# One late exponential per pair of key tiles, scores in groups of four, and one weight tile of 104 made without ScalarE

## The chip, the core and the metric

The kernel runs on one core of a Trainium2 chip. The metric is the device time of one execution in microseconds (us); of several runs the median is taken. The engines are called as in the profile: PE (TensorE matrix multiplication; PEld is its loading of weights), DVE (VectorE), ACT (ScalarE), POOL (GpSimd) and SP (SyncE, which issues nearly all DMAs here).

## What is computed

Four graph layers follow each other on 3327 nodes with 128 features, each of the form `x = x + layer(relu(layernorm(x)))`. Layers 0, 2 and 3 multiply by a 3327 x 3327 adjacency matrix of zeros and ones. Nearly all of the time goes to layer 1, an attention with a softmax for each of the 128 features:

```python
q = (x @ Wq.T).reshape(d, n, h)      # d = 128 softmaxes, n = 3327 nodes, h = 8
k = (x @ Wk.T).reshape(d, n, h)
v = (x @ Wv.T).reshape(d, n, h)
a = jnp.einsum('dnh,dmh->dnm', q, k) * scale
a = a + spatial_encoding + edge_encoding     # both are adj
a = jax.nn.softmax(a, axis=2)
out = jnp.einsum('dnm,dmh->dnh', a, v)
```

So 128 matrices of 3327 x 3327 exponentials are needed, `exp(q.k + 2 adj)`. The kernel calls each of the 128 a head.

## The kernel before

**Tiles.** Keys lie in 26 tiles of 128 partitions (`T = 26`), queries in seven chunks of 476 columns (`QW`; the last has 471), heads in 32 groups of four. The attention loop runs over chunks, in them over groups, in them over key tiles: 7 x 32 x 26 = 5824 steps, 2912 pairs of an even and an odd step. The order of the instructions on every engine is that of the code (a manual schedule), and each engine works through its own in that order; it stops at the first that has to wait.

**A step** (`scores`, then `weigh` of the step four before, `ahead = 4`). For each of four heads PE multiplies 32 rows (8 features in split precision) of keys and queries into a score tile of 128 keys x 476 queries in PSUM (L547). The four heads use four different groups of 32 rows of the array. Twice the adjacency (`a2`, bf16) is then brought in by one of three ways, named by a letter in `WAYS`:

- D: VectorE adds `a2` to the score tile and writes it to the weights `p8` (L552). These tiles are called `early`; four PSUM buffers of that name are used in turn. ScalarE takes the exponential of all five D tiles of a pair with one wide instruction of 5 x 476 columns (L557), in the odd step.
- I: PE adds `a2` to the score tile itself by a product with an identity matrix (L550), and ScalarE takes the exponential straight from PSUM (L553).
- G: ScalarE takes the exponential of the scores alone from PSUM (L553), and GpSimd multiplies by a stored `exp(a2)` (L555).

The I and G tiles are called `late`. An even step has the ways D D D I and one late tile, an odd one D D I G and two; each kind has one PSUM buffer (`late1`, `late2`, three banks in all). With four banks for `early` and one for the sum, the eight banks are full. A score matmul that writes `late` waits until ScalarE has read the last one there.

**Weighing.** `weigh` multiplies the four weight tiles of a step by the values (L564), each into its own group of 32 columns of the array, and sums over the key tiles in one PSUM bank. In the trace it shows as eight matmul records for a step, two passes for each head. After the last key tile VectorE copies the sum out (L573).

**Beside it.** The next group's keys, queries and values are loaded at step 4 (`load_heads`, L392), GpSimd casts two key tiles at a time from step 13 on (`key_pair`, L419). In the first chunk GpSimd also splits keys and queries of later groups into two parts (`Parting`). While one chunk is worked on, the adjacency of the next is loaded, doubled by GpSimd (L272), and stored; in a chunk's last group ScalarE makes the 13 tiles of its exponential (L347).

**Before attention** PE projects `q`, `k` and `v` for 26 row tiles; ScalarE copies them to staging buffers (`qk_st` L466, `v_st` L474), and SP stores them to DRAM. GpSimd sets a column of ones in each `v_st` first (L473). Between the rows a list `early` of prepared steps is worked off, among them the parting of groups 0 and 1 and the whole loading of the first four heads in one step.

Of the kernel before, what the change touches and what calls it, by code (L numbers as in the profile page):

```python
# [1 line left out]

# [6 lines left out]
F32 = mybir.dt.float32  # L9
F32R = mybir.dt.float32r  # L10
# [3 lines left out]
I32 = mybir.dt.int32  # L14
U32 = mybir.dt.uint32
AF = mybir.ActivationFunctionType
ALU = mybir.AluOpType
# [4 lines left out]
P = 128  # L22
N = 3327
D = 128
T = 26
NP = P * T
NH = 128
E = 8
EA = E + 1
HL = 2 * E  # L30
GP = NP * NH
QW = 476
# [22 lines left out]
def kernel(  # L55
# [23 lines left out]
    nc = tc.nc  # L79
# [183 lines left out]
    a_first = []  # L263
# [74 lines left out]
    kq = ctx_at.enter_context(tc.tile_pool(name="at_kq", bufs=2))  # L338
    e_pool = ctx_at.enter_context(tc.tile_pool(name="at_e", bufs=T // 2 + 1))

    def even(c):
        w = q_chunks[c][1]
        return w + w % 2

    def exp_of(a2, c):
        e = e_pool.tile([P, QW], F32, name="e")
        nc.scalar.activation(e[:, : even(c)], a2[:, : even(c)], AF.Exp)  # L347
        return e
# [7 lines left out]
    class Parting:  # L356


        def __init__(self, g):
            self.g, self.hi, self.lo = g, [None] * 2, [None] * 2  # L360
# [22 lines left out]
        def at(self, t):  # L383

            for side in range(2):
                t0 = 2 + 4 * side
                if t0 <= t < t0 + 4:
                    self.part(side, t - t0)
                if t == 11:
                    self.store(side)  # L390

    def load_heads(c, g):  # L392
        q0, w = q_chunks[c]
        k_in = kq.tile([P, NP], F32, name="k_in", bufs=1)
        q4 = kq.tile([P, QW], F32R, name="q4")
        v4 = kq.tile([P, 4, T, EA], F32, name="v4")
        nc.gpsimd.memset(k_in[:, N:], 0.0)
        if w % 2:
            nc.gpsimd.memset(q4[:, w : w + 1].bitcast(F32), 0.0)
        for i in range(4):  # L400
            n0 = (4 * g + i) * N
            for j in range(2):
                r = 32 * i + HL * j
                nc.sync.dma_start(k_in[r : r + HL, :N], kt[:, n0 : n0 + N])
                nc.sync.dma_start(q4[r : r + HL, :w].bitcast(F32), dram(qt, E * j * GP + n0 + q0, [[0, 2], [GP, E], [1, w]]))
        for i in range(4):
            n0 = (4 * g + i) * N
            nc.sync.dma_start(
                v4[:, i].rearrange("p t e -> p (t e)"),
                vd[n0 : n0 + NP, :].rearrange("(p t) e -> p (t e)", t=T),  # L410
            )
        return k_in, q4, v4, []

    def key_pair(heads):

        k_in, _, _, pairs = heads
        t = 2 * len(pairs)
        k = kq.tile([P, 2, P], F32R, name="k", bufs=T)
        nc.gpsimd.tensor_copy(k, slots(k_in)[:, t : t + 2, :])  # L419
        pairs.append(k)  # L420

    with tc.tile_pool(name="l1", bufs=1) as pool, tc.tile_pool(name="l1_ps", bufs=3, space=PSUM) as ps:
# [13 lines left out]
        st = ctx_st.enter_context(tc.tile_pool(name="l1_st", bufs=4))  # L436
# [7 lines left out]
        early = []  # L444
        for g in range(2):
            part = Parting(g)
            for side in range(2):
                early.append(lambda part=part: (part.load(0), part.load(1)) if part.lo[0] is None else None)
                early.append(lambda part=part, side=side: [part.part(side, i) for i in range(4)] and part.store(side))
        first, e_first = [], []  # L450
        early.append(lambda: first.extend(load_heads(0, 0)))
        ahead_part = Parting(2)
        early.append(lambda: (ahead_part.load(0), ahead_part.load(1)))
        early.append(lambda: e_first.extend(exp_of(a, 0) for a in a_first[1::2]))
        early += [lambda: (key_pair(first), key_pair(first))] * (T // 4)
        if T // 2 % 2:
            early.append(lambda: key_pair(first))
        for r in range(T):
            kp = rows_of(r)
            lhs = hT[:, r * P : r * P + kp]  # L460
            for i, (dst, mx) in enumerate(((qf, q_max), (kf, k_max))):
                pp = ps.tile([P, 2, 512], F32, name="pp", bufs=2)
                for c in range(2):
                    nc.tensor.matmul(pp[:kp, c, :], lhs, w_st[:, i, c * 512 : c * 512 + 512], start=True, stop=True)
                s = st.tile([P, E * NH], F32, name="qk_st")
                nc.scalar.activation(s[:kp], pp[:kp].rearrange("p a b -> p (a b)"), AF.Copy, scale=D**-0.5 if i == 0 else 1.0)  # L466
                nc.vector.tensor_reduce(mx[:kp, r : r + 1], s[:kp], AX.X, ALU.max, apply_absolute_value=True)
                store(dst[:E].rearrange("e (r c) -> r e c", c=NH), s.rearrange("p (e c) -> p e c", c=NH), r, kp)
            pp = ps.tile([P, 2, 512], F32, name="pp", bufs=2)
            for c in range(2):  # L470
                nc.tensor.matmul(pp[:kp, c, :], lhs, w_st[:, 2, c * 512 : c * 512 + 512], start=True, stop=True)
            s = st.tile([P, NH, EA], F32, name="v_st")
            nc.gpsimd.memset(s[:, :, E : E + 1], 1.0)  # L473
            nc.scalar.copy(s[:kp, :, :E], pp[:kp].rearrange("p a (c e) -> p (a c) e", e=E))  # L474
            store(vd.rearrange("(r c) e -> r (c e)", c=NH), s.rearrange("p c e -> p (c e)"), r, kp)

            if r > 1 and early:
                early.pop(0)()
# [23 lines left out]

    WAYS = ("DDDI", "DDIG")
    PLACES = ((0, 1, 2, 5), (3, 4, 6, 7))
    two_i = const.tile([P, P], BF16, name="two_i")
    nc.vector.tensor_copy(two_i, ident)
    engines = {
# [5 lines left out]
    }  # L515
    n_groups = NH // 4
    ahead = 4
    adj_pools.append(ctx_at.enter_context(tc.tile_pool(name="at_adj1", bufs=T)))
    with tc.tile_pool(name="at_in", bufs=1) as a_pool, tc.tile_pool(name="at_p", bufs=3) as p_pool, tc.tile_pool(
        name="at_ps", bufs=1, space=PSUM  # L520
# [12 lines left out]
            q0, w = q_chunks[c]  # L533
            nc.sync.dma_start(adj16[t][:, q0 : q0 + w], a2[:, :w])

        def scores(step, heads, a2, e_a, p8):
            c, _, t = step
            we = even(c)
            _, q4, _, pairs = heads
            ways, places = WAYS[t % 2], PLACES[t % 2]  # L540
            n_d = ways.count("D")
            late = ps.tile([P, 4 - n_d, 512], F32, name=f"late{4 - n_d}")
            early = [ps.tile([P, 512], F32, name="early", bufs=4) for _ in range(n_d)]
            for i in (*range(n_d, 4), *range(n_d)):
                r = slice(32 * i, 32 * i + 32)
                sp = early[i] if i < n_d else late[:, i - n_d]
                nc.tensor.matmul(sp[:, :we], pairs[t // 2][r, t % 2, :], q4[r, :we], start=True, stop=ways[i] != "I")  # L547
            for i in range(4):
                if ways[i] == "I":
                    nc.tensor.matmul(late[:, i - n_d, :we], two_i, a2[:, :we], start=False, stop=True)  # L550
            for i in range(n_d):
                nc.vector.tensor_tensor(p8[:, places[i], :we], early[i][:, :we], a2[:, :we], op=ALU.add)  # L552
            nc.scalar.activation(p8[:, places[n_d] : places[3] + 1, :we], late[:, :, :we], AF.Exp)  # L553
            if ways[3] == "G":
                nc.gpsimd.tensor_tensor(p8[:, places[3], :we], p8[:, places[3], :we], e_a[:, :we], op=ALU.mult)  # L555
            if t % 2:
                nc.scalar.activation(p8[:, :5, :we], p8[:, :5, :we], AF.Exp)  # L557

        def weigh(step, v4, p8):
            c, g, t = step  # L560
            q0, w = q_chunks[c]
            kp = rows_of(t)
            for i in range(4):
                nc.tensor.matmul(  # L564
                    acc[32 * i : 32 * i + EA, :w],
                    v4[:kp, i, t, :],
                    p8[:kp, PLACES[t % 2][i], :w],
                    start=(t == 0),
                    stop=(t == T - 1),
                )  # L570
            if t == T - 1:
                o4 = a_pool.tile([P, QW], F32, name="o4")
                nc.vector.tensor_copy(o4[: 96 + EA, :w], acc[: 96 + EA, :w])  # L573
                for i in range(4):
                    n0 = (4 * g + i) * N + q0
                    nc.sync.dma_start(ot[:, n0 : n0 + w], o4[32 * i : 32 * i + EA, :w])

        with tc.manual_schedule(engines=engines):
            groups = [(c, g) for c in range(len(q_chunks)) for g in range(n_groups)]
            steps = [(c, g, t) for c, g in groups for t in range(T)]  # L580
            heads = first
# [4 lines left out]
            for j, step in enumerate(steps):  # L586
# [6 lines left out]
                        a_t, a_next = a_next, []  # L593
                        e_t, e_next = e_next, []
                if t % 2 == 0:
                    p8 = p_pool.tile([P, 8, QW], F32, name="p8")
                scores(step, heads, a_t[t], e_t[t // 2], p8)
                begun[j] = (step, heads[2], p8)
                if j >= ahead:
                    weigh(*begun.pop(j - ahead))  # L600
                if t == min(4, T // 2) and more:
                    coming = load_heads(*groups[n])
                if c == 0 and g + 2 < n_groups:
# [506 lines left out]
```

## Time and profile before

| | us |
|---|---|
| runs, median (lowest to highest of 3) | 11194.51 (11192.19 to 11195.0) |
| the profiled execution | 11195.14 |
| its span, first to last instruction | 11193.4 |
| attention in it: first exponential to last | 576 to 10471 |
| projection before it | 380 to 566 |

The profile is one execution. Of a group of equal instructions it gives the busy time, the mean duration of one and the idle time of its engine in front of them. Durations contain a start and a tail that overlap with the neighbours (two late exponentials and a wide one have means of 980, 1387 and 2609 ns, and yet they start again every 3.37 us), so throughput is read from start to start. PE's matmuls are pipelined and their ends are modelled; for PE, too, starts are what counts. PE's clock was granted in full during attention.

POOL's groups that matter: the product with `exp(a2)` takes 1212 ns, a cast of two key tiles 697 ns, doubling a tile with a tensor_scalar 1417 ns.

### The profile page before, as it was taken

To read this page: it belongs to the slowest core of one execution; us is meant where nothing else is said; L and a number is where in the kernel's file an instruction comes from. 1 tells how busy PE (TensorE), PEld (TensorE's weight loads), DVE (VectorE), ACT (ScalarE), POOL (GpSimd) and SP (SyncE) were. 2 spreads that over 40 slices of the span, in tenths; PEclk is the share of its full clock that TensorE was granted. 3 is DMA by queue.
4 is the path that set the end of the run, shared out by engine and by line. 5 is a ranking of instruction groups with operands and counts; after the bars stand their busy time and mean duration, and the time that the engine had idled before them with its cause. 6 is when DMAs were issued, how large, how long until landed. Compare 5 with 4: busy or idle time off the path is not lost. (4 is left out here: it accounts for less than half of the span.)

```text
span 11193.4 us, 209350 instructions
## 1 busy us (share of the span) xinstructions
PE 10850.5 (97%) x79530; PEld 3005.9 (27%) x79530; DVE 9343.1 (83%) x15429; ACT 10199.3 (91%) x9152; POOL 6016.3 (54%) x6964
## 2 busy tenths in 40 slices
PE   9899999999999999999999999999999999999996
PEld 4322222222222222222222222222222222222453
DVE  8588888888888888888888888888888888888656
ACT  0399999999999999999999999999999999999522
POOL 0277777555555555555555555555555555555203
PEclk9899999999999999999999999999999999999998
DMA  7755554333333333333333333333333332333432
GB/s 264 238 129 120 123 127 109 65 64 64 68 64 62 67 66 63 68 65 61 68 66 63 66 66 61 67 66 61 66 66 61 66 63 55 61 58 58 135 113 97
DMA packets 417541, 942.25 MB, mean 84 GB/s; under 512 B 67936, under 2 KB 345937, under 8 KB 380940
## 3 DMA queue, kind: packets, MB, share of 16 engines
q1 hardware_dynamic: 412762, 918.98, 37.4%
q8 instruction: 627, 10.27, 0.4%
q0 software_dynamic: 3760, 9.78, 0.3%
q14 instruction: 392, 3.21, 0.1%
HBM read 788.78 MB, written 139.71 MB: 83 GB/s over the span
## 5 line engine op out<-in xcount | busy, mean ns | idle before, releaser
L552 DVE TENSOR_TENSOR p<-early,a 128x476 f32<-128x476 f32 (+1 forms) x14560 | 8426.4, 646 | 1369.4 <-PE early L547 1297.5
L557 ACT ACTIVATE p<-p 128x2380 f32<-128x2380 f32 (+1 forms) x2912 | 7568.4, 2599 | 0.4
L564 PE MATMUL acc<-p,v 128*9 128x476 f32 (+1 forms) x46592 | 5748.5, 564 | 15.3 <-ACT p L557 1.4
L553 ACT ACTIVATE p<-late 128x476 f32<-128x476 f32 (+1 forms) x5824 | 5315.4, 1175 | 13.8 <-DMA q<-qt 10.2
L555 POOL TENSOR_TENSOR p<-p,e 128x476 f32<-128x476 f32 (+1 forms) x2912 | 3528.1, 1212 | 3204.3 <-ACT p L553 2998.6
L547 PE MATMUL late<-q,k 32*128 32x476 f32 (+1 forms) x8736 | 2798.2, 478 | 99.5 <-ACT p L553 39.7
L547 PE MATMUL early<-q,k 32*128 32x476 f32 (+1 forms) x14560 | 2843.6, 478 | 9.4 <-DVE p L552 9.4
L419 POOL CAST k<-k_in 128x256 fp32r<-128x256 f32 x2912 | 1936.5, 697 | 886.4 <-DMA k_in<-kt 339.4
L547 PEld LDWEIGHTS late<-q,k 32*128 32x128 f32 x8736 | 1065.4, 181 | 4890.4 <-ACT p L553 4186.2
L550 PE MATMUL late<-a,two_i 128*128 128x476 bf16 (+1 forms) x5824 | 2180.8, 374 | 0.0
L547 PEld LDWEIGHTS early<-q,k 32*128 32x128 f32 x14560 | 1113.0, 181 | 9.9 <-DVE p L552 9.9
L564 PEld LDWEIGHTS acc<-p,v 128*9 128x9 f32 x46592 | 695.2, 88 | 1272.6 <-issue 1185.8
L550 PEld LDWEIGHTS <-two_i 128*128 128x128 bf16 x5824 | 556.2, 96 | 1329.0 <-issue 1329.0
L189 ACT COPY agg<-agg_ps 128x512 f32<-128x512 f32 x15 | 8.2, 591 | 485.5 <-PE agg_ps L204 290.6
L230 PE MATMUL agg_ps<-a,part 128*128 128x512 bf16 (+1 forms) x1092 | 227.0, 369 | 4.3 <-ACT agg L928 3.2
L272 POOL TENSOR_SCALAR a<-a_in 128x476 bf16<-128x476 f32 (+2 forms) x156 | 221.1, 1417 | 0.5
L272 POOL TENSOR_SCALAR a<-a 128x476 bf16<-128x476 f32 (+1 forms) x26 | 36.4, 1400 | 288.1 <-DMA a<-in_adjT_dram 288.1
L923 PE MATMUL sp<-yT,hT 128*128 128x512 f32 (+1 forms) x364 | 170.7, 610 | 12.3 <-ACT agg L928 6.4
L204 PE MATMUL agg_ps<-a,h 128*128 128x512 f32 (+2 forms) x364 | 148.2, 570 | 26.2 <-DVE h L164 26.2
L573 DVE COPY o<-acc 105x476 f32<-105x476 f32 (+1 forms) x224 | 144.5, 645 | 4.6 <-PE acc L564 4.6
L204 PE MATMUL agg_ps<-a,x 128*128 128x512 f32 (+2 forms) x364 | 145.3, 562 | 0.6 <-ACT x L318 0.6
L230 PEld LDWEIGHTS <-part 128*128 128x128 f16 x1092 | 108.6, 99 | 117.7 <-issue 10.3
(236 smaller groups left out, 2592.0 us busy)
## 6 DMA issues: line engine op xcount, KB each, us to landing
k_in<-kt SPq DMA_DIRECT2D x1792, 207.9 KB
v<-vd SPq DMA_DIRECT2D x896, 117.0 KB
a<-in_adjT_dram SPq DMA_DIRECT2D x50, 1663.5 KB
a<-adj SPq DMA_DIRECT2D x78, 831.8 KB
q<-qt SPq DMA_DIRECT2D x1536, 29.8 KB
a_in<-in_adjT_dram SPq DMA_DIRECT2D x125, 238.0 KB
adj<-a SPq DMA_DIRECT2D x156, 119.0 KB
vd<-v_st SPq DMA_DIRECT2D x25, 576.0 KB
```

The costliest lines, as they stand in the source:

```text
L204: nc.tensor.matmul(acc[c][:, :w], lhs[:kp, t, :], a[:kp, c0 : c0 + w], start=(t == 0), stop=(t == T - 1))
L230: nc.tensor.matmul(acc[c][:, :w], part[:, t, :], a[:, c0 : c0 + w], start=(t == 0 and i == 0), stop=(t == T - 1 and i == len(parts) - 1),)
L272: nc.gpsimd.tensor_scalar(a2[:kp, :w], a, 2.0, None, op0=ALU.mult)
L419: nc.gpsimd.tensor_copy(k, slots(k_in)[:, t : t + 2, :])
L547: nc.tensor.matmul(sp[:, :we], pairs[t // 2][r, t % 2, :], q4[r, :we], start=True, stop=ways[i] != "I")
L550: nc.tensor.matmul(late[:, i - n_d, :we], two_i, a2[:, :we], start=False, stop=True)
L552: nc.vector.tensor_tensor(p8[:, places[i], :we], early[i][:, :we], a2[:, :we], op=ALU.add)
L553: nc.scalar.activation(p8[:, places[n_d] : places[3] + 1, :we], late[:, :, :we], AF.Exp)
L555: nc.gpsimd.tensor_tensor(p8[:, places[3], :we], p8[:, places[3], :we], e_a[:, :we], op=ALU.mult)
L557: nc.scalar.activation(p8[:, :5, :we], p8[:, :5, :we], AF.Exp)
L564: nc.tensor.matmul(acc[32 * i : 32 * i + EA, :w], v4[:kp, i, t, :], p8[:kp, PLACES[t % 2][i], :w], start=(t == 0), stop=(t == T - 1),)
L923: nc.tensor.matmul(sp[:, c0 : c0 + w], slots(zT)[:, t, :], z2T[:, cols], start=True, stop=False)
```

## The change

In the attention loop a pair of steps is now built at once:

- The pair has one `late` tile of three banks, and one exponential over its three tiles (3 x 476 columns) in place of two. The head with way I of the even step is now head 0.
- The eight score matmuls stand in two groups of four (`FOURS`): first four D tiles (heads 1, 2, 3 of the even step and head 0 of the odd one), then the even step's `weigh`, then the three late tiles and the fifth D tile, then both identity products. Each four uses the four row groups once. The odd step's `weigh` follows.
- VectorE's adds stand right behind their matmuls in the program; `early` keeps its four buffers, taken in turn by five tiles a pair.
- From the second chunk on, one of the 104 weight tiles of each group (head 1 of key tile 1, `SPARE`) leaves the wide exponential of the group's first pair, which then has four tiles. Its sum of scores and `a2` goes to a buffer of its own. In later steps GpSimd splits it into a multiple of ln 2 and a rest (five instructions at steps 4, 6, 8, 10, 12), and VectorE works out a polynomial of degree five and multiplies by the power of two (five instructions at steps 13, 15, 18, 21, 24). `weigh` leaves the tile out at step 1 and adds it at step 25, ahead of that head's own matmul.

Around it: the pool of cast key tiles has 20 buffers for 26; the loading of the first four heads is cut into eight pieces worked off between the rows of the projection, with casts and exponentials spread as well; four fixed `v_st` buffers get their column of ones once, before the rows.

```diff
-        k = kq.tile([P, 2, P], F32R, name="k", bufs=T)
+        k = kq.tile([P, 2, P], F32R, name="k", bufs=T // 2 + 7)
...
-        early.append(lambda: first.extend(load_heads(0, 0)))
...
-        early.append(lambda: e_first.extend(exp_of(a, 0) for a in a_first[1::2]))
-        early += [lambda: (key_pair(first), key_pair(first))] * (T // 4)
...
+        pieces, e_first = [], []
+        first = load_heads(0, 0, pieces)
+        early += pieces[:4]
...
+            def step(i=i):
+                for f in pieces[4 + i : 5 + i if i < key_steps - 1 else None]:
+                    f()
+                for n in (2 * i, 2 * i + 1):
+                    if n < T // 2:
+                        key_pair(first)
+                        e_first.append(exp_of(a_first[2 * n + 1], 0))
...
+        v_sts = [st.tile([P, NH, EA], F32, name=f"v_st{i}", bufs=1) for i in range(4)]
+        for s in v_sts:
+            nc.gpsimd.memset(s[:, :, E : E + 1], 1.0)
...
-            s = st.tile([P, NH, EA], F32, name="v_st")
-            nc.gpsimd.memset(s[:, :, E : E + 1], 1.0)
+            s = v_sts[r % 4]
...
-    WAYS = ("DDDI", "DDIG")
-    PLACES = ((0, 1, 2, 5), (3, 4, 6, 7))
+    WAYS = ("IDDD", "DDIG")
+    PLACES = ((5, 0, 1, 2), (3, 4, 6, 7))
+
+    FOURS = (((0, 1), (0, 2), (0, 3), (1, 0)), ((0, 0), (1, 2), (1, 3), (1, 1)))
...
+    SPARE = (1, 1)
...
+                if t == 4:
+                    nc.gpsimd.tensor_scalar(k, x, 1.0 / LN2, ROUND, op0=ALU.mult, op1=ALU.add)
+                elif t == 6:
+                    nc.gpsimd.tensor_scalar(r, k, -ROUND, -LN2, op0=ALU.add, op1=ALU.mult)
+                elif t == 8:
+                    nc.gpsimd.tensor_tensor(r, r, x, op=ALU.add)
+                elif t == 10:
+                    nc.gpsimd.tensor_scalar(k.bitcast(I32), k, 127.0 - ROUND, 2.0**23, op0=ALU.add, op1=ALU.mult)
+                elif t == 12:
+                    nc.gpsimd.tensor_scalar(x, r, POLY[4], None, op0=ALU.mult)
+                elif t in (13, 15, 18, 21):
+                    nc.vector.scalar_tensor_tensor(x, x, POLY[(21, 18, 15, 13).index(t)], r, op0=ALU.add, op1=ALU.mult)
+                elif t == 24:
+                    nc.vector.scalar_tensor_tensor(r, x, 1.0, k, op0=ALU.add, op1=ALU.mult)
...
+        def scores(step, heads, a2s, between, spare):
...
+            late = ps.tile([P, 3, 512], F32, name="late")
+            for n, four in enumerate(FOURS):
+                if n == 1:
+                    between()
+                for odd, i in four:
+                    way, place = WAYS[odd][i], PLACES[odd][i]
+                    sp = ps.tile([P, 512], F32, name="early", bufs=4) if way == "D" else late[:, place - 5]
+                    r = slice(32 * i, 32 * i + 32)
+                    nc.tensor.matmul(sp[:, :we], pairs[t // 2][r, odd, :], q4[r, :we], start=True, stop=way != "I")
+                    if way == "D":
+                        dst = spare.x if spare and (odd, i) == SPARE else p8[:, place]
+                        nc.vector.tensor_tensor(dst[:, :we], sp[:, :we], a2s[odd][:, :we], op=ALU.add)
+            for odd, i in FOURS[1]:
+                if WAYS[odd][i] == "I":
+                    nc.tensor.matmul(late[:, PLACES[odd][i] - 5, :we], two_i, a2s[odd][:, :we], start=False, stop=True)
+            nc.scalar.activation(p8[:, 5:, :we], late[:, :, :we], AF.Exp)
+            n_d = 4 if spare else 5
...
+            nc.scalar.activation(p8[:, :n_d, :we], p8[:, :n_d, :we], AF.Exp)
...
+                if spare and (t, i) == SPARE:
+                    continue
+                out = acc[32 * i : 32 * i + EA, :w]
+                if spare and (t, i) == (T - 1, SPARE[1]):
+                    nc.tensor.matmul(out, v4[:, i, SPARE[0], :], spare.r[:, :w], start=False, stop=False)
...
+                        spare = Spare() if c else None
```

## The prediction

> **What bounds the kernel now.** I read the page's first two parts (which engine is full, and where), then the windows of the attention stage, then the groups by form and the waits inside it, then one pair of key tiles in the timelines.
>
> ```profile
> PE 10850.5 (97%) x79530; PEld 3005.9 (27%) x79530; DVE 9343.1 (83%) x15429; ACT 10199.3 (91%) x9152; POOL 6016.3 (54%) x6964
> ```
> ```profile
> 3400.00:4810.00 1410.00, 1393.47 (x10785) 342.58 (x10777) 1215.88 (x2105) 1410.00 (x1257) 794.47 (x887) 1.00 0.34 65
> ```
> ```profile
> L557 ACT ACTIVATE p<-p 128x2380 f32<-128x2380 f32 x1764 | 4602.7, 2609 | 0.1
> L553 ACT ACTIVATE p<-late 128x952 f32<-128x952 f32 x1764 | 2446.1, 1387 | 0.1
> L553 ACT ACTIVATE p<-late 128x476 f32<-128x476 f32 x1763 | 1727.2, 980 | 0.0
> ```
> ```profile
> PEld late L547 <- ACT p L553: 2558.4, 3012, 1.4
> DVE p L552 <- PE early L547: 788.6, 1557, 1.4
> ```
>
> Attention lies between 576 us (the first exponential) and 10471 us: 9895 us for 2912 pairs of key tiles (7 chunks x 32 groups x 13). In a whole chunk (second line; columns: length, busy PE, PEld, DVE, ACT, POOL) ScalarE is busy all 1410 us, and its exponentials wait for nothing (0.1 us in 6000). PE waits for ScalarE's late tiles, VectorE for PE. So ScalarE is the bound; PE's 97% is modelled and has to be counted by starts. One pair, by engine:
>
> ```profile
> 6002.93 1.55 ACT L553 ACTIVATE p<-late 128x476 f32<-128x476 f32 x2
> 6004.22 2.34 ACT L557 ACTIVATE p<-p 128x2380 f32<-128x2380 f32 x1
> 6006.30 1.57 ACT L553 ACTIVATE p<-late 128x476 f32<-128x476 f32 x2
> ...
> 6003.68 0.48 PE L547 MATMUL early<-q,k 32*128 32x476 f32 x3
> 6004.10 0.38 PE L550 MATMUL late<-a,two_i 128*128 128x476 bf16 x1
> 6004.40 0.98 PE L564 MATMUL acc<-p,v 128*9 128x476 f32 x8
> 6005.32 0.48 PE L547 MATMUL late<-q,k 32*128 32x476 f32 x2
> 6005.73 0.37 PE L550 MATMUL late<-a,two_i 128*128 128x476 bf16 x1
> 6006.04 0.99 PE L564 MATMUL acc<-p,v 128*9 128x476 f32 x8
> 6007.06 0.48 PE L547 MATMUL late<-q,k 32*128 32x476 f32 x1
> ...
> 6004.32 2.90 DVE L552 TENSOR_TENSOR p<-early,a 128x476 f32<-128x476 f32 x5 [0.49 <-PE early L547]
> ```
>
> ScalarE, start to start: both late exponentials 1.29, the wide one 2.08, together 3.37 us. 2912 x 3.37 = 9813; 78 exponentials of the next chunk's adjacency at 0.49 are 38; the other 44 us are ramps and small waits. PE: scores to identity 0.42, identity to weighing 0.30, weighing to scores 0.91 unwaited, 1.64 us a step, 3.27 a pair: only 0.1 us under ScalarE. VectorE: five adds every 0.56 us, the last lasting 0.64; 2.90 us of work, then 0.5 idle.
>
> **What the skill says.** "ScalarE: Activation LUTs", What ACT_TABLE_LOAD costs: 0.833 ns per element plus a fixed cost, part of it overlapped by the next. The trace agrees with the slope: 1428 late elements are 1.19 of the 1.29 us, 2380 wide ones 1.98 of 2.08. So the fixed part is 0.05 for each late exponential and 0.10 for the wide one, where the page's figures (186 less 93) leave 0.09; I use the trace. "TensorE: Matmul & The Clock Gate", step 1: weights load ahead of running matmuls when row groups don't conflict. It agrees where one kind follows itself (the 1092 bf16 products at L230, mean width 475, each with its own load, take 227.0 us: 0.21 each), while every change of kind above costs about 0.1 more than its columns. "SBUF — State Buffer", SBUF: two separate sides: a VectorE instruction with two SBUF inputs and a GpSimd one exclude each other. No run here shows it, since the adds read PSUM.
>
> **The change, part by part.**
>
> *ScalarE.* One late exponential of 1428 columns for two: -0.05 us a pair, period 3.32. In six chunks one group of 13 pairs has one wide exponential of 1904 columns: -0.40 us a group, 192 groups. If nothing else is late: 2912 x 0.05 = 146 and 192 x 0.40 = 76, so -222 us.
>
> *PE's work.* Per pair it becomes scores, weighing, scores, identity, identity, weighing. No row shows scores straight to weighing; I take scores to identity, 0.42 (bounds 0.30 for no switch, 0.52 for the switch that weighing to scores pays). Identity to identity is 0.20. Sum 0.42 + 0.91 + 0.42 + 0.20 + 0.30 + 0.91 = 3.16: 0.1 less than now.
>
> *The new ring.* What decides is the order in fours with four `early` buffers. Five tiles a pair go through four buffers in turn, so the fourth matmul of a pair's first four takes the buffer of the fifth tile of the pair before: PE stands until VectorE's last add has finished, with both weighings and the other four queued behind. Before, that buffer was asked for a step (1.64 us) later, after a weighing. From the first four's start to the fourth matmul of the next pair: 0.64 (6003.68 to 6004.32, a start with three waits, as it stays) + 2.90 (five adds) + 0.05 (at the ramp an add ends at 576.83 and the matmul that waits for it starts at 576.88) = 3.59. From that matmul round to the next first four: 0.38 (a lone one instead of four, from 0.42) + 0.91 + 0.42 + 0.20 + 0.30 + 0.91 = 3.12. This path spans two pairs: (3.59 + 3.12) / 2 = 3.36 us a pair. PE would wait 0.2 us there while VectorE idles 0.5; ScalarE at 3.32 would be the one with slack. Against 3.37 now: 2912 x -0.01 = -29 us. Bounds by the unknown switch, half of -0.12 to +0.10 a pair: 3.30 (then ScalarE's 3.32 holds) to 3.41.
>
> *The spare tile on PE.* Weighing runs four column groups side by side. Leaving out one of four at t=1 shortens nothing; the extra one at t=25 shares its column group with head 1's own, so that weighing lasts two more passes of 0.40, +0.81 us. In a ring that binds it counts: the first four that follow it start 0.81 later; two pairs later the other half of the ring has absorbed at most 0.2 (the wait for the fourth matmul). So 0.6 to 0.8, taken 0.7: 192 x 0.7 = +134 us.
>
> *The spare tile on VectorE and GpSimd.* Five two-operand steps a group on VectorE, each about an add (0.56), in the gap of 3.36 - 2.81 = 0.55: nothing, if started at once; each start that falls on a GpSimd instruction waits up to its 1.2 us. By the starts above, GpSimd's product begins 4.1 us after a pair's first four and is followed by two casts (0.63 each), so it rests from 3.1 to 4.1 us after the next one, and the step arrives at 3.5. I take 0, bounds 0 to +1.2 for two in five: 0 to +92 us. GpSimd's five steps (tensor_scalar 1.4 at L272, product 1.2) come to 6.8 us a group of 44 in pairs where it casts nothing. The first polynomial step waits for GpSimd's at t=12, done about 3.3 us into the pair, 0.2 before it is wanted. The smaller `k` pool (20 for 26) is reused only after its reader: a group's eighth tile takes the first tile of the group before, 20 steps old. Nothing.
>
> *Before attention.* The 380 to 566 us window holds 186 us for 26 rows at a pace of 5.15 us (134): stores fill the queue, and loading the first heads in one go leaves ScalarE idle for 18 us at 478. Splitting those loads over rows, and setting the ones column once in four buffers (POOL waits 102 us for stores there, mostly beside the work), moves the same bytes: -10 us, bounds +5 and -25.
>
> Sum: -29 + 134 + 0 - 10 = +95. The profiled execution took 11195.14 us (span 11193.4 and 1.7 around it), 0.6 above the median of the runs, so the prediction on the median is 11290.
>
> **Rivals.**
>
> *ScalarE stays the bound.* For it: it alone never waits now, and PE's sum falls by 0.1. It needs a ring under 3.32, thus 0.08 less over its 6.71 us. Then -146 - 76 - 10: about 10965. Against it: the ring's parts are measured starts except two.
>
> *A wash.* The ring holds, but the wait swallows the extra weighing, or casual gains before attention match it: -29 - 10 and half of 134, about 11200.
>
> *The shared port.* The ring holds and the polynomial steps do meet GpSimd: at two in five, 192 x 5 x 0.4 x 1.2 = 460 us if each waited in full, half of that on average: 11290 + 230 = 11520. It decides only if the steps arrive 0.7 us earlier or later than worked out.
>
> **Chances.** Ring with the extra weighing 0.42; ScalarE bound 0.36; wash 0.12, most of it no change; shared port 0.10. What this kernel's measurement can tell from no change is about 0.2% (22 us). From these: slower 0.52, the same 0.11, faster 0.37. The likeliest case alone: 11215 to 11385. The range takes in ScalarE's case below and part of the port's above: 10960 to 11430.
>
> **What will show it.** Right: the fourth early matmul starts 0.2 us after the three before it, waiting for VectorE; ScalarE's late exponentials get idle time; pairs at 3.36 in the first chunk and dearer in the other six, by 0.6 to 0.8 us a group. Wrong: ScalarE without idle time and 3.32 us in the first chunk, with cheaper groups afterwards; the first four followed by weighing after 0.3 us; or polynomial steps far over 0.65 us.

## The result, and the profile after

| | us |
|---|---|
| before, median of 4 runs on the same chip | 11194.76 (11192.19 to 11196.85) |
| after, median of 4 runs | 11537.89 (11532.35 to 11547.75) |
| ratio | 1.0308, 95% interval 1.0295 to 1.0321 |
| forecast | 11290, range 10960 to 11430 |

The changed kernel is slower by 343 us, on the side forecast as the likelier one, but by 3.6 times the 95 us of the sum. First the page of the kernel after: the engine line and, out of its costliest groups, three.

```profile
PE 11176.2 (97%) x79530; PEld 3145.6 (27%) x79530; DVE 10026.2 (87%) x16389; ACT 10112.7 (88%) x6240; POOL 7047.7 (61%) x7902
...
L615 ACT ACTIVATE p<-p 128x2380 f32<-128x2380 f32 (+2 forms) x2912 | 6277.7, 2156 | 0.0
L612 ACT ACTIVATE p<-late 128x1428 f32<-128x1428 f32 (+1 forms) x2912 | 3957.3, 1359 | 453.2 <-PE late L611 394.3
L587 DVE SCALAR_TENSOR_TENSOR spare_x<-spare_x,spare_r 128x476 f32<-128x476 f32 (+1 forms) x768 | 656.2, 854 | 6.4 <-POOL spare_x L585 6.2
```

ScalarE, which waited for nothing before, now idles 453 us in front of its late exponentials, 394 of them for PE's identity product. It is no longer the bound. And the polynomial steps of L587 last 854 ns on average, where the prediction had taken each for about as long as an add (0.56 us) and the five for no cost at all. "Polynomial steps far over 0.65 us" stood there as a sign of being wrong. The windows of the first chunk and of a later one (columns: length, busy PE, PEld, DVE, ACT, POOL, clock, DMA share, GB/s):

```profile
576.00:1990.00 1414.00, 1400.19 (x10764) 343.95 (x10756) 1213.51 (x2100) 1400.20 (x839) 1064.22 (x1365) 1.00 0.50 118
3400.00:4810.00 1410.00, 1389.32 (x10374) 351.92 (x10371) 1277.90 (x2179) 1344.24 (x812) 935.24 (x1011) 1.00 0.33 62
```

In the later chunk, which has the spare tile, 10374 PE instructions pass in 1410 us, 4% fewer than the 10785 before; in ScalarE's 1410 us are now 66 of idle time. By the starts of the wide exponential the first chunk lasts 1422.7 us (1417.9 before) and the next five 1470 to 1476 (1416 before): nearly everything is lost where the spare tile is.

The timeline of the first chunk after (columns: start, length, engine, line, operation, tiles, count, idle before):

```profile
1199.84 0.49 PE L605 MATMUL early<-q,k 32*128 32x476 f32 x4
1200.45 2.89 DVE L608 TENSOR_TENSOR p<-early,a 128x476 f32<-128x476 f32 x5 [0.73 <-PE early L605]
...
1203.02 0.85 PE L605 MATMUL early<-q,k 32*128 32x476 f32 x4
1203.40 0.18 PEld L605 LDWEIGHTS early<-q,k 32*128 32x128 f32 x1 [0.19 <-DVE p L608]
1203.63 2.89 DVE L608 TENSOR_TENSOR p<-early,a 128x476 f32<-128x476 f32 x5 [0.29 <-PE early L605]
```

Here the ring of the prediction can be read off: the first four start at 1199.84, the five adds end at 1203.34, and the fourth matmul of the next pair starts at 1203.40, behind three that started at 1203.02. From there it is 3.16 us to the following first four (1206.56). 3.56 + 3.16 = 6.72 for two pairs, against 3.59 + 3.12 = 6.71 in the working. The fourth matmul is late in every second pair only, by 0.38 us; in the pairs between it starts with the other three (1199.84).

The rest needs a finer look. The table gives, from the traces, the mean time from the wide exponential of one pair of a group to that of the next pair, over the groups of the second to sixth chunk (each chunk's last group left out); the pairs of a group are numbered 0 to 12. It already holds experiments told below; "merge" is the change without the spare tile.

| us | 1 to 2 | 9 to 10 | 10 to 11 | 11 to 12 | mean of the other nine | sum of 13 |
|---|---|---|---|---|---|---|
| before | 3.38 | 3.42 | 3.39 | 3.38 | 3.39 | 44.05 |
| after | 4.50 | 3.85 | 3.70 | 3.51 | 3.37 | 45.91 |
| merge only | 3.71 | 3.43 | 3.34 | 3.40 | 3.36 | 44.14 |
| merge only, sum not copied | 3.37 | 3.40 | 3.38 | 3.36 | 3.37 | 43.83 |
| merge only, first touch of `p8` | 3.65 | 3.39 | 3.35 | 3.32 | 3.33 | 43.65 |
| after, no extra weighing | 3.72 | 4.06 | 3.73 | 3.49 | 3.38 | 45.39 |
| after, no polynomial | 4.50 | 3.45 | 3.35 | 3.40 | 3.36 | 44.94 |
| after, all steps early | 4.50 | 3.39 | 3.39 | 3.36 | 3.37 | 44.93 |

Two places of the group are dear: pair 1 to 2, where the group's border is weighed, and pairs 9 to 12, where the last polynomial steps stand.

### The profile page after: what moved, and what is told of

Same layout as the page of the kernel before. It is cut to its first block, busy times and chain, and to the rows that moved or that the text cites. A ratio compares the mean times of both kernels' runs of the same rounds, so it can differ in the third digit from the quotient of the medians.

```text
span 11536.6 us, 208149 instructions
## 1 busy us (share of the span) xinstructions
PE 11176.2 (97%) x79530; PEld 3145.6 (27%) x79530; DVE 10026.2 (87%) x16389; ACT 10112.7 (88%) x6240; POOL 7047.7 (61%) x7902
## 5 line engine op out<-in xcount | busy, mean ns | idle before, releaser
L615 ACT ACTIVATE p<-p 128x2380 f32<-128x2380 f32 (+2 forms) x2912 | 6277.7, 2156 | 0.0
L633 PE MATMUL acc<-p,v 128*9 128x476 f32 (+2 forms) x46208 | 5933.4, 565 | 83.1 <-DVE o L642 82.0
L612 ACT ACTIVATE p<-late 128x1428 f32<-128x1428 f32 (+1 forms) x2912 | 3957.3, 1359 | 453.2 <-PE late L611 394.3
L605 PE MATMUL early<-q,k 32*128 32x476 f32 (+1 forms) x14560 | 3370.7, 480 | 53.5 <-DVE p L608 49.6
L605 PEld LDWEIGHTS early<-q,k 32*128 32x128 f32 x14560 | 1403.9, 182 | 2649.9 <-DVE p L608 2563.8
L611 PE MATMUL late<-a,two_i 128*128 128x476 bf16 (+1 forms) x5824 | 1679.0, 370 | 0.0
L605 PE MATMUL late<-q,k 32*128 32x476 f32 (+1 forms) x8736 | 1416.4, 479 | 29.1 <-ACT p L612 28.7
L633 PEld LDWEIGHTS acc<-p,v 128*9 128x9 f32 (+1 forms) x46208 | 752.2, 88 | 2039.1 <-issue 1880.6
L605 PEld LDWEIGHTS late<-q,k 32*128 32x128 f32 x8736 | 548.0, 181 | 2358.7 <-issue 1502.6
L587 DVE SCALAR_TENSOR_TENSOR spare_x<-spare_x,spare_r 128x476 f32<-128x476 f32 (+1 forms) x768 | 656.2, 854 | 6.4 <-POOL spare_x L585 6.2
L585 POOL TENSOR_SCALAR spare_x<-spare_r 128x476 f32<-128x476 f32 (+1 forms) x192 | 268.7, 1399 | 0.0
```

Source lines behind the costliest of these rows:

```text
L585: nc.gpsimd.tensor_scalar(x, r, POLY[4], None, op0=ALU.mult)
L587: nc.vector.scalar_tensor_tensor(x, x, POLY[(21, 18, 15, 13).index(t)], r, op0=ALU.add, op1=ALU.mult)
L605: nc.tensor.matmul(sp[:, :we], pairs[t // 2][r, odd, :], q4[r, :we], start=True, stop=way != "I")
L611: nc.tensor.matmul(late[:, PLACES[odd][i] - 5, :we], two_i, a2s[odd][:, :we], start=False, stop=True)
L612: nc.scalar.activation(p8[:, 5:, :we], late[:, :, :we], AF.Exp)
L615: nc.scalar.activation(p8[:, :n_d, :we], p8[:, :n_d, :we], AF.Exp)
```

## The experiments

Edits are against the kernel after. Theory: the ring of PE and VectorE binds (PE's fourth early matmul waits for VectorE's last add, the next adds wait for PE's scores), and what is added to it at the two places makes the time. Rivals: ScalarE is still the bound; the extra weighing alone makes the loss; the polynomial steps lose time by their length and not by meeting GpSimd. The kernel before, run beside the experiments, had medians of 11189.70 to 11194.06 us, so differences of about 5 us between runs say nothing.

**The merge alone.**

```diff
-                        spare = Spare() if c else None
+                        spare = None
```

> The changed kernel without the spare tile: all chunks are built as its first chunk is. Ring theory (a path over two pairs through PE and VectorE's five adds sets 3.36 us a pair; the wait of the next group's first weighing for the copied sum costs 0.36 us a group; everything else that was lost belongs to the spare tile): each chunk takes what the first takes in the changed kernel, 1423 us, so 11537.9 less about 306 us: 11232 us, a little slower than before. ScalarE theory (ScalarE still sets the pairs where there is no spare tile): 0.05 us less a pair than before, about 11040 us, and no idle time of ScalarE.

Measured: 11200.93 us (11197.74 to 11204.34), ratio 1.0006 (0.9997 to 1.0015). That is 31 us under the ring's 11232, and 161 over ScalarE's 11040, whose case is out. So the merge wins nothing that can be measured, and the spare tile costs the other 337 us. But the ring should have given about 11156 (-29 and -10): 45 us are missing, and by the table the place to look is pair 1 to 2, 3.71 us although no extra weighing is there.

**ScalarE relieved further.** The merge alone with `n_d = 4` in every pair: the exponential of each fifth D tile is left out, 0.40 us of ScalarE a pair.

```diff
-            n_d = 4 if spare else 5
+            n_d = 4
```

> As the run without the spare tile, and in every pair the wide exponential covers four tiles, not five; the fifth tile's exponential is left out. It takes 0.40 us a pair off ScalarE and nothing else. Ring theory: no change, within 30 us of the run without the spare tile, ScalarE idle by 0.4 us more a pair. ScalarE theory: 0.15 to 0.4 us a pair less, 430 us or more.

Measured: 11172.23 us, ratio 0.9982 (0.9974 to 0.9990). ScalarE has some 1160 us less to do (2912 x 0.40) and 29 us are gained. Its waits between 3000 and 9000 us (total us, times, longest):

```profile
PEld early L605 <- DVE p L608: 1558.7, 2555, 0.8
...
ACT p L612 <- PE late L611: 511.3, 1060, 1.3
```

PE's loads for an early matmul wait for VectorE's adds, and ScalarE waits for PE: the ring, with 3.18 and 3.55 us in turn from pair to pair.

**The last add, later or not.** The merge alone, with a VectorE memset of 192 columns in each pair, once in front of the fifth add (in the ring) and once behind it (off the ring).

```diff
+                        if (odd, i) == (1, 1):
+                            nc.vector.memset(pad, 0.0)
                         nc.vector.tensor_tensor(dst[:, :we], sp[:, :we], a2s[odd][:, :we], op=ALU.add)
```

> As the run without the spare tile, with a memset of 192 columns on VectorE between the fourth and the fifth add of each pair (0.24 us by the rate of the 512-column memset, 0.485 us). VectorE idles 0.5 us a pair, so by its busy time there is room. Ring theory: the fifth add, and with it the fourth matmul of the next pair, comes 0.24 us later, which costs half of that a pair: +0.12 us, +350 us. If VectorE's idle time were real slack: no change.

> The same memset behind the fifth add, in the 0.5 us in which VectorE waits for the next pair's first four. Ring theory: it is off the ring, within 30 us of the run without the spare tile. If VectorE's amount of work were the limit: as much as with the memset ahead of the fifth add.

Measured: 11400.91 us in the ring (ratio 1.0185, 1.0164 to 1.0205) and 11204.31 off it (1.0008, 0.9999 to 1.0018). The same instruction costs 200 us or 3, so the path runs through the end of the last add. The 350 expected was too much: the memset moves the add by 0.21 us, but the add behind it then lasts 0.59 in place of 0.64, so the ring grows by 0.157, half of which falls to a pair: 2912 x 0.078 = 228.

**The copy of the sum.** The merge alone, with the buffer of a group's sum filled with ones in place of the copy from PSUM; the sums are left out of the output.

```diff
-                nc.vector.tensor_copy(o4[: 96 + EA, :w], acc[: 96 + EA, :w])
+                nc.vector.memset(o4[: 96 + EA, :w], 1.0)
```

> Merge alone (as in e1_merge_only), but VectorE fills the group's sum buffer with ones instead of copying it out of PSUM, so the sums are left out of the output. With that neither VectorE waits for the last weighing of a group nor PE for the copy. Copy theory: in the merged order the next group's first weighing stands right behind the first four and waits for the copy; without it pair 1 to 2 of a group falls from 3.71 us to about 3.35, 224 x 0.36 = 80 us, so 11120 us (11110 to 11140) against 11201. Rival, the dear pair comes from something else at the group's border (the new group's keys, queries or values, a DMA): pair 1 to 2 stays near 3.7 and the time near 11200.

Measured: 11130.89 us, ratio 0.9949 (0.9935 to 0.9963), 70 us less than the merge alone; pair 1 to 2 falls to 3.37. Some 4 of the 70 us lie in the kernel before, which was that much faster beside this run (11189.70 against 11194.06). The copy is what the prediction had not seen. In the timeline after, at a group's border:

```profile
4023.56 0.49 PE L605 MATMUL early<-q,k 32*128 32x476 f32 x4
4023.73 0.65 DVE L642 COPY o<-acc 105x476 f32<-105x476 f32 x1 [0.93 <-PE acc L633]
...
4024.43 1.08 PE L633 MATMUL acc<-p,v 128*9 128x476 f32 x8 [0.38 <-DVE o L642]
```

There is one PSUM bank for the sum. The new group's first weighing stands 0.42 us behind the first four and could start at 4023.98; it waits for the copy until 4024.43. The adds, too, stand behind the copy on VectorE: in the merge alone the first of them starts 0.73 us after its scores at this place, for 0.62 elsewhere. The run takes both away, so it prices the copy and not PE's wait alone. In the order before, scores and an identity product stood between (0.72 us), and all but 0.13 us of PE's wait was hidden: 3.38 at that place.

**Without the extra weighing.** The extra matmul at t=25 is left out, and with it the spare tile's part of the sum.

```diff
-                if spare and (t, i) == (T - 1, SPARE[1]):
+                if False:
```

> The changed kernel with its spare tile, but without the extra weighing matmul of the spare tile at the last step; that tile's share of the sum is left out, all other steps on VectorE and GpSimd stay. Ring theory: the pair after which it came falls from 4.5 to 3.7 us, 0.8 us a group: 11537.9 less 154: 11385 us. If PE had room for it: no change.

Measured: 11425.22 us, ratio 1.0209 (1.0189 to 1.0230). 113 us less than after: pair 1 to 2 gives back 0.78 us, but 9 to 10 rises from 3.85 to 4.06. The time is 40 us over the 11385 expected: the polynomial steps take longer in this run (what they last over 643 ns adds up to 213 us, against 185 in after; why is open). Against the merge alone 224 us remain, so the extra weighing is not all.

**Without the polynomial.** VectorE's five steps are left out; the spare tile is weighed with what GpSimd made of it.

```diff
-                elif t in (13, 15, 18, 21):
+                elif False:
...
-                elif t == 24:
+                elif False:
```

> The changed kernel with its spare tile, but without VectorE's five polynomial steps a group; the tile is weighed with what GpSimd leaves, so the exponential of that tile is left out. GpSimd's five steps and the extra weighing stay. If the polynomial steps cost what the pairs of their places show (about 0.9 us a group): 11537.9 less 173: 11365 us. If the cost lies in GpSimd's steps or in the weighing: over 11500.

Measured: 11355.41 us, ratio 1.0147 (1.0127 to 1.0167): 182 us less than after. Pairs 9 to 12 go back to 3.45, 3.35 and 3.40. So five VectorE steps a group, counted at nothing, cost 182 us. By length or by meeting GpSimd? The timelines after, GpSimd's first and then VectorE's:

```profile
4000.45 1.32 POOL L430 CAST k<-k_in 128x256 fp32r<-128x256 f32 x2 [3.38 <-DMA adj<-a]
4001.70 1.24 POOL L621 TENSOR_TENSOR p<-p,e 128x476 f32<-128x476 f32 x1
...
4008.19 1.31 POOL L430 CAST k<-k_in 128x256 fp32r<-128x256 f32 x2
```

```profile
3998.54 0.64 DVE L587 SCALAR_TENSOR_TENSOR spare_x<-spare_x,spare_r 128x476 f32<-128x476 f32 x1
...
4009.25 0.76 DVE L587 SCALAR_TENSOR_TENSOR spare_x<-spare_x,spare_r 128x476 f32<-128x476 f32 x1
```

The step at 4009.25 ends at 4010.01, 0.51 after the casts' end at 4009.50. Over the whole trace, 460 steps started with GpSimd at rest and last 643 ns in the median (631 to 658); of the 500 others 481 end 0.507 to 0.520 us after the end of a GpSimd instruction (all of them 0.468 to 0.601), whatever was left of it. That is the exclusive lock of the Trainium skill, "SBUF — State Buffer", SBUF: two separate sides; this trace agrees. The lines also show when GpSimd rests: it stands 3.38 us for the next group's keys to arrive, and the step at 3998.54 falls there. (The line names another transfer, but the cast reads only the keys; at the same place of a group the trace of before names them, see below.) From 4000.45 on it catches up, one instruction behind the other, and the steps that come then meet it. The steps' means are 653 and 641 ns for the first two and 1280, 843 and 763 for those at t=18, 21 and 24. What all 960 last over 643 ns adds up to 185 us, close to the 182.

A few of these waits are very long. One step at t=18, the matmul of PE that waits behind it, and the stretch after that (columns as in the windows above):

```profile
2116.07 5.08 DVE L587 SCALAR_TENSOR_TENSOR spare_x<-spare_x,spare_r 128x476 f32<-128x476 f32 x1
...
2121.76 0.76 PE L605 MATMUL early<-q,k 32*128 32x476 f32 x1 [3.76 <-DVE p L608]
```
```profile
2121.20:2127.90 6.70, 6.14 (x27) 1.25 (x27) 5.25 (x10) 3.44 (x2) 2.91 (x4) 0.50 0.00 0
```

At the end of this standstill PE's clock, granted in full before, went to 0.50 for 6.8 us. That happens at ten places of the attention, 61 us together, among them each of the eight at which PE stood for more than 2 us; before, without the polynomial and with all steps early it never happens there. At half speed 61 us are worth up to 31, an estimate. So a part of what the steps cost may come through the clock, as a consequence of the long waits; no run separates the two.

**Most steps early.** GpSimd's five at t=2, 3, 3, 3 and 5, VectorE's first four at 6, 8, 10 and 12, the last left at 24.

```diff
-                if t == 4:
+                if t == 2:
...
-                elif t in (13, 15, 18, 21):
+                elif t in (6, 8, 10, 12):
```

> The changed kernel with the spare tile's steps earlier in the group: GpSimd's at key tiles 2, 3 (three of them) and 5, VectorE's first four at 6, 8, 10 and 12, where GpSimd casts no keys; the last stays at 24. Shared port theory (a step of VectorE with two SBUF operands stands until the running GpSimd instruction ends): the two dear steps go, 0.6 to 0.8 us a group: 115 to 155 us less, about 11400 us. If the steps cost because VectorE has no room for 0.56 us a pair: no change, since there are as many.

Measured: 11552.38 us, ratio 1.0326 (1.0309 to 1.0344), a miss by 150. The same two views of this kernel, GpSimd's and VectorE's:

```profile
4006.85 1.32 POOL L430 CAST k<-k_in 128x256 fp32r<-128x256 f32 x2
4008.11 1.22 POOL L619 TENSOR_TENSOR p<-p,e 128x476 f32<-128x476 f32 x1
4009.26 0.69 POOL L430 CAST k<-k_in 128x256 fp32r<-128x256 f32 x1
```

```profile
4007.26 3.20 DVE L587 SCALAR_TENSOR_TENSOR spare_r<-spare_x,spare_k 128x476 f32<-128x476 f32 x1
...
4026.91 0.64 DVE L585 SCALAR_TENSOR_TENSOR spare_x<-spare_x,spare_r 128x476 f32<-128x476 f32 x1
```

The four moved steps are short, 0.64, but the one left at 24 can wait for several GpSimd instructions in a row: this one ends at 4010.46, again 0.51 after an end, that of the last cast (4009.95). Of the 192, 38 last over 3 us. One step a group then costs 199 us (11552.38 less the 11353.27 of the next run), more than all five did. Its length over 643 ns adds up to only 129 us; but the granted clock is 0.50 for 150 us of this attention, in 30 stretches, which may be worth up to 75 more (an estimate).

**All steps early.** As the last one, with the last step at t=14 too.

```diff
-                elif t == 24:
+                elif t == 14:
```

> As the kernel with the earlier spare steps, and VectorE's last step, too, moved from key tile 24 to 14, so that all five stand where GpSimd rests when they start. In the kernel with the earlier steps the first four took 0.64 us each and the last 3.2. Shared port theory: all five take 0.64, the group loses nothing to them, and the time is that of the run without polynomial steps, 11355, or up to 30 us more. Theory that VectorE has no room for five more instructions: about 11540 as before.

Measured: 11353.27 us, ratio 1.0146 (1.0129 to 1.0163): 185 us under after and within 2 us of the kernel without the steps. All 960 last 0.635 to 0.656 us. The same work costs nothing where it does not meet GpSimd: the cost comes from the meeting, not from the 0.64 us of a step.

**Memsets in place of the steps.** After, with each polynomial step replaced by two memsets of 476 columns, which do not read SBUF.

```diff
-                    nc.vector.scalar_tensor_tensor(x, x, POLY[(21, 18, 15, 13).index(t)], r, op0=ALU.add, op1=ALU.mult)
+                    nc.vector.memset(x, 0.0)
+                    nc.vector.memset(x, 0.0)
```

> The changed kernel with each of VectorE's five polynomial steps replaced in its place by two memsets of 476 columns (0.3 us each by the start-to-start time of the 192-column memset, 0.14), which read nothing from SBUF; the exponential of the spare tile is left out. Shared port theory: as long on VectorE, but no waiting for GpSimd: 11355 to 11385 us. Theory that VectorE has no room: about 11540.

Measured: 11714.97 us, ratio 1.0469 (1.0448 to 1.0489), a miss. In its timeline:

```profile
4001.28 0.46 DVE L587 MEMSET spare_x<- 128x476 f32 x1
4001.91 0.46 DVE L588 MEMSET spare_x<- 128x476 f32 x1 [0.17 <-PE early L607]
4002.28 2.83 DVE L610 TENSOR_TENSOR p<-early,a 128x476 f32<-128x476 f32 x5
```

Two memsets on one buffer, the second behind the first, hold VectorE for 1.0 us (4001.28 to 4002.28), not the 0.6 meant, and the gap is 0.55. So the run does not tell lock from length at the size in question. That it is 360 us slower than the kernel without the steps fits with what exceeds the gap being paid for in the ring, but does not show it.

**The merge with a first touch.** The merge alone with a memset of one column at the head of each pair, so that VectorE's waits for `p8` to come free are taken ahead of the first add.

```diff
+            nc.vector.memset(p8[:, 0, :1], 0.0)
```

> The changed kernel without the spare tile, with a memset of one column on VectorE at the head of each pair, into the pair's weight buffer ahead of its first add. The memset takes over the waits for GpSimd, ScalarE and the old weighing, so that the first add has one wait (for its scores) in place of three. Ring theory: VectorE's start after the scores falls from about 0.62 us by the 0.1 us that the two extra waits take, half of it a pair, until ScalarE's 3.32 us a pair sets the time: up to 0.05 us a pair, 11200.9 less 100 to 140: about 11080 us, faster than before. If the time between the two matmuls of the ring is made by PE alone (or if the memset is itself late): no change, 11200.

Measured: 11093.44 us (11083.46 to 11097.65), ratio 0.9910 (0.9893 to 0.9926). This version is faster than both kernels. Its timeline:

```profile
4002.51 0.65 PE L606 MATMUL early<-q,k 32*128 32x476 f32 x4
4002.78 0.06 DVE L597 MEMSET p<- 128x1 f32 x1 [0.15 <-PE acc L634]
4003.03 2.89 DVE L609 TENSOR_TENSOR p<-early,a 128x476 f32<-128x476 f32 x5 [0.20 <-PE early L606]
...
4004.00 0.19 PEld L606 LDWEIGHTS late<-q,k 32*128 32x128 f32 x3 [0.80 <-ACT p L613]
```

The memset waits for the weighing that frees the buffer, and the adds now start 0.52 us after the first four, for 0.61 in the ring's timeline above. That takes 0.09 off 6.73 us: 3.32 a pair. And PE's late matmul waits for ScalarE again (4004.00). Most pairs run at 3.32, the 3.32 worked out for ScalarE.

**Both together.** All steps early, with the first touch.

> All five spare steps early and the memset of one column at the head of each pair: the spare tile under the best conditions found. ScalarE theory of the spare tile's worth: 0.40 us a group less on ScalarE, which sets the pairs once the ring is shortened: 11093.4 less up to 76 us. Ring theory: the extra weighing still costs 0.6 to 0.8 us a group, more than ScalarE saves: 11150 to 11250 us, slower than the same kernel without the spare tile.

Measured: 11451.66 us, ratio 1.0234 (1.0217 to 1.0251), a miss. In its timeline:

```profile
4003.28 0.64 DVE L585 SCALAR_TENSOR_TENSOR spare_x<-spare_x,spare_r 128x476 f32<-128x476 f32 x1
4003.87 0.06 DVE L595 MEMSET p<- 128x1 f32 x1
4004.05 2.90 DVE L607 TENSOR_TENSOR p<-early,a 128x476 f32<-128x476 f32 x5
```

From step to next step (4003.28 to 4006.86) are 3.58 us without a gap: 0.59 for the step, 0.18 for the memset, 2.81 for five adds. In the five pairs with a step VectorE itself is now the bound. The touch pays only where VectorE has the room.

## Why the prediction was wrong

The sum was 95 us and the loss 343. The kernels in a row from before to after, each term the difference of two neighbours (so the terms must add up to the loss):

| us | predicted | measured | by |
|---|---|---|---|
| merge, ring, before attention | -39 | -64 | sum not copied, against before |
| the copy of the sum | not seen | +70 | merge only, less sum not copied |
| spare tile without the polynomial: extra weighing, GpSimd's five steps, shorter exponential | +134 | +154 | no polynomial, less merge only |
| polynomial steps on VectorE | 0 | +182 | after, less no polynomial |

- **The failed step: the five polynomial steps, "I take 0, bounds 0 to +1.2 for two in five: 0 to +92 us".** The mechanism was on record, as the wait for GpSimd, also as a rival at 11520, close to where the time came out. The closeness is partly luck: that rival had 230 us for the steps, which cost 182, and nothing for the copy, which cost 70. Misjudged was the place. "It rests from 3.1 to 4.1 us after the next one" holds where GpSimd keeps pace, and was taken for all pairs. The first two steps do come while it rests. The three later ones come while it catches up after a wait for the next group's keys, without a rest. That wait was in the trace of before, right in front of the pair at 6003.68 from which the prediction read its starts (timeline there, GpSimd):

```profile
5999.16 1.32 POOL L419 CAST k<-k_in 128x256 fp32r<-128x256 f32 x2 [3.55 <-DMA k_in<-kt]
6000.42 1.23 POOL L555 TENSOR_TENSOR p<-p,e 128x476 f32<-128x476 f32 x1
...
6006.39 1.36 POOL L419 CAST k<-k_in 128x256 fp32r<-128x256 f32 x2
```

  From 5999.16 to 6007.75 GpSimd has no rest there. That the cost is the meeting was shown by moving the steps (182 us less without them, 185 less with all of them where GpSimd rests). The upper bound was wrong by itself: 192 x 0.4 x 1.2 = 92 counts one step a group where there are five; the rival's own 460 had them all. With these as the upper bound, the sum's upper end is 11750 and holds the result.
- **The step left out: the copy of the sum.** The new neighbours, scores and then weighing, were priced for what PE's switch costs; what a group's first weighing itself waits for was not asked. In a ring that binds, 70 us. Before, an identity product stood in front of the weighing and hid most of the wait.
- **The ring: right.** 6.71 us for two pairs forecast, 6.72 and 6.73 measured; the fourth early matmul waited for VectorE as foretold, though by 0.38 us in every second pair and not by 0.2 in each. The unknown switch, scores to weighing, was taken as 0.42 and is 0.42 (the weighing behind the first four at 1199.84 starts at 1200.26). The first rival, ScalarE the bound, fell with the merge alone. Its condition was right too: "a ring under 3.32, thus 0.08 less over its 6.71 us". The first touch took 0.09 away, and that kernel came out 1% faster than the merge alone.
- **The extra weighing: right in kind, a little short.** 0.7 us a group taken of 0.6 to 0.8; 4.50 against 3.72 is 0.78, and of the 154 us in the table 152 lie at this pair (4.50 against 3.71, 192 times), so little is left for GpSimd's steps. Terms do not simply add here: with the polynomial in place, leaving the weighing out gives back only 113. The polynomial steps then wait 28 us longer (213 for 185), most of the difference of 41.
- **Before attention: right.** -10 us forecast; the first wide exponential starts at 572.5 us, 6.6 earlier than before (579.1).
- GpSimd's tensor_scalar steps were taken at 1.4 us each; three of the four take 0.59 and one 1.40. It decided nothing.

Left open: the mean is worst at t=18, where eight of the nine steps over 3 us stand, but why was not tried apart from the timeline, and neither was a run with GpSimd's wait for keys taken away. How much of the steps' cost is the halved clock is not known. That the touch acts through the number of waits on the first add is read from its timeline; no run counts waits.

## What to carry to other kernels

Where a step is put into an idle gap of one engine and shares SBUF with another, look at the other engine over the whole period of the loop, above all behind its longest wait: after a wait it works without rests, and a gap that is free in the quiet pairs is not free there. When instructions are reordered, ask for each moved one what it waits for itself (a bank, a copy), not only what the switch costs. And when two engines wait for each other in a ring, a tenth of a microsecond in front of one instruction can be worth more than a large saving elsewhere (here 107 us, against 29 for 1160 us less work on ScalarE).

## What the hardware showed unexpectedly

- A VectorE polynomial step, with two SBUF inputs, that starts while GpSimd works mostly ends 0.507 to 0.520 us after the end of a GpSimd instruction, and can stand through several of them (5.08 and 3.20 us for 0.64).
- In the attention of the kernel after, PE stood eight times for 2.5 to 3.9 us; within about 2 us of the end of each, its clock went to 0.50 for 3.4 or 6.8 us.
- A one-column memset ahead of the first add, which probably takes over part of its waits, brought its start 0.09 us closer to PE's matmul; with it the merge won 107 us (11200.93 to 11093.44).
- GpSimd's tensor_scalar from f32 to f32 took 0.59 us with two operations (L577, L579) and 1.40 with one (L585).
